# First query–key row by feature chunks, an aligned big buffer and earlier third-slice weights in a graph-attention layer

## The chip, the cores and the metric

One Trainium2 chip; the kernel runs on one core. The metric is the device time of one execution, in microseconds, as the median of the runs. The unchanged kernel took 2683.31 us (three runs, 2682.59 to 2688.69).

## The reference

A pre-norm graph attention layer over 128 graphs of 128 nodes with 768 features, 12 heads of 64:

```
h = relu(layernorm(x))                       # x: [128, 128, 768]
q, k, v = h @ Wq + bq, h @ Wk + bk, h @ Wv + bv
scores = q k^T / sqrt(64) + beta * adj       # per head
scores = where(adj > 0, scores, -9e15)
out = x + softmax(scores) v
```

Everything is float32.

## The kernel before

**Groups and slices.** Four graphs form a group (32 groups). For each group the projections are done in three slices in this order: `qk0` (features 0 to 383 of q and k), `v` (all of v) and `qk1` (features 384 to 767 of q and k). For groups 1 to 31 each slice is done as 15 products of sums of blocks (`product_z`, line 559 holds its matmuls): its weight operands (`T...`) were prepared once, most are kept in DRAM (`kept_...`) and streamed back for each group, eleven stay resident. Group 0 is done plainly (`plain_slice`, matmuls on line 855) from the raw weights, and while it runs VectorE (DVE) and GpSimd (POOL) prepare the operands of the products (`prepare`, lines 283 to 326: `sums` on lines 305 and 307, `rest` on lines 284 to 293, which also stores the operand to DRAM).

**Raw weights.** One big SBUF buffer, `sbig` (line 168), holds the raw q and k weights of the first slice in its first half, the raw v weights in its second half, then the first two graphs of x and a 128x128 identity and averaging matrix. A weight load covers 32 partitions (a quarter, index `a`), so each set of columns takes four DMAs (`load_cols`, line 229). Before the change the first slice is loaded by column block j, 128 columns of all 768 features at a time: per DMA 32 partitions of six 512-byte runs, 96 KB (`raw_qk`, lines 238 to 244, called on lines 344, 345 and 347). The q part of block 0 goes out on the SyncE queue (SP), its k part on the ScalarE queue (ACT), all the rest on SP. The load of graphs 2 and 3 (`load_x(0, 1)`) stands between block 1 and block 2. When the first slice is done, its half of `sbig` is overwritten with the raw weights of the third slice, in eight DMAs (`raw_qk1_piece`, line 246), one each at slots 5 to 12 of the `v` slice (line 1058). A slot is one (row, j, k) step of `plain_slice`; a slice of group 0 has 18.

**The first slice of group 0.** Row r is a pair of graphs (256 columns), j a block of 128 output features of q and of k, k one of three chunks of 256 input features. Each (r, j, k) is four matmuls of q and k, and three k's accumulate in one pair of PSUM banks; there are four such pairs (`take`, `give`). Before the change row 0 goes j by j: j = 0 with all three k's for graph 0, then the same for graph 1, then j = 1 and j = 2 for both graphs. Graphs 0 and 1 are normalized by rows (`rows_1`, `rows_2`: statistics, scaling on DVE, transposes on TensorE line 925, ReLU on ACT line 931). Graphs 2 and 3 are normalized by moments: statistics on DVE (line 364), a first matmul with the averaging matrix (`moments_1`, line 375), a few small DVE operations, a second one (`moments_2`, line 389), a power on POOL (line 396) and the shift (398), then scaling on DVE and ACT (456, 450), and three 32x32 block transposes on DVE (471) that make the operands A10, A11, A12 of row 1. `second` (line 952) turns the biases (three small DMAs on ACT, lines 947 to 949; transpose on TensorE line 957) and is issued in the midst of j = 0.

**Order.** In this first slice the order is the program's with some `issue_after` ties; from the second slice on the order is written out by hand (`manual_schedule`, line 1052) through `then(slot, ...)`. `fill` (line 937) issues matmuls of the identity with itself while TensorE has nothing to do yet: 15 at the start and 1, 1 and 7 after the transposes of graph 0 (`FILL`, line 107).

Of the kernel before, what the change touches and what calls it, by code (L numbers as in the profile page):

```python
# [106 lines left out]
FILL = (1, 1, 7)  # L107
# [21 lines left out]
def direct(ctx, tc, x, adj, wq, bq, wk, bk, wv, bv, beta, out, bad):  # L129
# [36 lines left out]
    RAW = NC * 6 * P  # L166
    sbig = const.tile([P, 2 * RAW + 2 * D + 2 * P], F32, name="sbig")

# [36 lines left out]
    nhalf = const.tile([P, 1], F32, name="nhalf")  # L205
# [3 lines left out]
    tiny = const.tile([P, 1], F32, name="tiny")  # L209
# [3 lines left out]

    NS = 2 * NG + 1
    seen = const.tile([P, NS], F32, name="seen")

# [12 lines left out]
    def load_cols(engine, t, name, at, chunks=slice(0, NC)):  # L229
        for a in range(NB):  # L230
            engine.dma_start(t[a * SQ:(a + 1) * SQ], rows_of[name][a][:, chunks, at:at + t.shape[-1]])

# [5 lines left out]
    def raw_qk(u, t, parts, engines=(nc.sync, nc.sync)):  # L238

        v = t.rearrange("p (c i j n) -> p c i j n", c=NC, i=2, j=3)  # L240
        for lo, hi in parts:
            for i, name in enumerate(("q", "k")):
                load_cols(engines[i], v[:, :, i, lo:hi].rearrange("p c j n -> p c (j n)"), name, (lo + 3 * u) * P)
        name_raw(u, v)
# [8 lines left out]
    def raw_v():  # L253
        t = flat(RAW, RAW + NC * 4 * P).rearrange("p (c n) -> p c n", c=NC)
        own = flat(RAW + NC * 4 * P, 2 * RAW).rearrange("p (c n) -> p c n", c=NC)
        load_cols(nc.sync, t, "v", 0)
        load_cols(nc.sync, own, "v", 4 * P)
        for k in range(3):
            for j in range(3):
                b = t[:, :, j * 2 * P:(j + 1) * 2 * P] if j < 2 else own  # L260
                wt["v", f"B{k}{j}"] = b[:, 2 * k:2 * k + 2].rearrange("p c (i n) -> p c i n", i=2)
# [95 lines left out]
    st, pm, rstd, shift = {}, {}, {}, {}  # L357
# [11 lines left out]
    def moments_1(G, lo, hi):  # L369
# [4 lines left out]
        for q in range(0, P, HD):  # L374
            nc.tensor.matmul(pm[G, lo][q:q + HD, 0], mean8.rearrange("p a i -> p (a i)")[:, q:q + HD],
                             halves(G, lo, hi, 1), start=True, stop=True)
# [8 lines left out]
    def moments_2(G, lo, hi, mean, d):  # L385

        n = hi - lo
        for q in range(0, P, HD):
            nc.tensor.matmul(pm[G, lo][q:q + HD, 1], mean8.rearrange("p a i -> p (a i)")[:, q:q + HD], d,
# [911 lines left out]
```

## Time and profile before

| | |
|---|---|
| median of three runs | 2683.31 us (2682.59 to 2688.69) |
| the profiled execution | 2680.71 us, of which the span from the first to the last instruction is 2678.9 us |
| TensorE busy | 2652.9 us, 99% of the span |
| VectorE, ScalarE, GpSimd busy | 2179.0, 1749.4 and 2072.5 us |
| granted TensorE clock | 0.998 of full speed over the span |
| DMA | 721.71 MB, mean 269 GB/s |

The profile is one execution. In a timeline row stand the start in us, the busy time in us, the engine, the source line, the operation, its output and inputs by name, the form and the count, and in brackets how long the engine sat idle before it and what released it. TensorE's matmuls are PE, its weight loads PEld, the DMA issues of SyncE and ScalarE SPq and ACTq. One float32 matmul shows as two PE rows. A row of a window table has the busy time (and the count) of each engine in one stretch, the granted clock, the mean busy share of the DMA engines, and GB/s.

### The profile page before, as it was taken

To read this page: it belongs to the slowest core of one execution; us is meant where nothing else is said; L and a number is where in the kernel's file an instruction comes from. 1 tells how busy PE (TensorE), PEld (TensorE's weight loads), DVE (VectorE), ACT (ScalarE), POOL (GpSimd) and SP (SyncE) were. 2 spreads that over 40 slices of the span, in tenths; PEclk is the share of its full clock that TensorE was granted. 3 is DMA by queue.
4 is the path that set the end of the run, shared out by engine and by line. 5 is a ranking of instruction groups with operands and counts; after the bars stand their busy time and mean duration, and the time that the engine had idled before them with its cause. 6 is when DMAs were issued, how large, how long until landed. Compare 5 with 4: busy or idle time off the path is not lost.

```text
span 2678.9 us, 121522 instructions
## 1 busy us (share of the span) xinstructions
PE 2652.9 (99%) x52051; PEld 2564.7 (96%) x52051; DVE 2179.0 (81%) x2701; ACT 1749.4 (65%) x4608; POOL 2072.5 (77%) x3043
## 2 busy tenths in 40 slices
PE   9999999999999999999999999999999999999998
PEld 8799999999999999999999999999999999999997
DVE  6877888878888788888788887788887888877885
ACT  2567766676666677666766666776667676667654
POOL 5877778877778777788777787777887777877774
PEclk9999999999999999999999999999999999999999
DMA  9888888989888998889898888988898988888875
GB/s 238 283 261 282 275 270 277 277 265 284 276 271 273 267 279 273 273 277 279 265 281 279 270 272 271 283 274 270 277 277 266 283 277 271 272 274 276 257 240 163
DMA packets 530341, 721.71 MB, mean 269 GB/s; under 512 B 105980, under 2 KB 374024, under 8 KB 529800
## 3 DMA queue, kind: packets, MB, share of 16 engines
q1 hardware_dynamic: 528640, 713.12, 86.7%
q8 instruction: 411, 6.73, 1.0%
q10 hardware_dynamic: 1160, 0.79, 0.2%
q14 instruction: 130, 1.06, 0.1%
HBM read 647.73 MB, written 66.05 MB: 266 GB/s over the span
## 4 chain that ended last, share of the span: by engine, by line
PE 45%; POOL 29%; ACT 13%; issue 5%; DMA 4%; DVE 3%; SPq 0%; POOLq 0%; ACTq 0%; DVEq 0%
PE pair L559 34%; PE pair L695 4%; POOL v L616 4%; PE pair L638 3%; POOL v L615 3%; PE pair L855 3%; POOL A L481 3%; POOL home L614 3%; ACT x L450 3%; ACT e L648 3%; POOL home L601 2%; POOL home L603 2%; ACT home L577 2%; ACT home L579 2%; POOL v L612 2%
## 5 line engine op out<-in xcount | busy, mean ns | idle before, releaser
L583 DVE TENSOR_TENSOR home<-home,pair 128x896 f32<-128x896 f32 x810 | 860.7, 1076 | 273.4 <-PE pair L559 220.7
L559 PE MATMUL pair<-sbig,T_qk 128*64 128x128 f32 x13020 | 833.0, 273 | 1.8 <-DVE sbig L476 0.9
L559 PEld LDWEIGHTS pair<-sbig,T_qk 128*64 128x64 f32 x13020 | 708.2, 137 | 11.6 <-issue 6.4
L559 PE MATMUL pair<-A,T_qk 128*64 128x128 f32 x6944 | 465.6, 273 | 0.4 <-ACT e L707 0.4
L601 POOL TENSOR_TENSOR home<-home 128x256 f32<-128x256 f32 x298 | 246.5, 827 | 268.6 <-DVE home L583 260.1
L678 ACT ACTIVATE e<-e,sm 128x64 f32<-128x64 f32 x1512 | 382.2, 346 | 109.5 <-DVE sm L666 109.5
L559 PE MATMUL pair<-T_v,sbig 128*64 128x128 f32 x6944 | 415.1, 274 | 0.6 <-DMA T_v<-kept_v 0.3
L695 PE MATMUL pair<-v,e 128*64 128x65 f32 x6048 | 401.7, 221 | 6.3 <-DVE e L646 5.9
L577 ACT ACTIVATE home<-pair 128x640 f32<-128x640 f32 x325 | 231.4, 712 | 262.5 <-PE pair L559 201.6
L559 PEld LDWEIGHTS pair<-T_v,sbig 128*64 128x64 f32 x6944 | 380.7, 137 | 12.9 <-issue 10.6
L559 PEld LDWEIGHTS pair<-A,T_qk 128*64 128x64 f32 x6944 | 377.2, 137 | 5.4 <-ACT e L707 4.8
L695 PEld LDWEIGHTS pair<-v,e 128*64 128x64 f32 x6048 | 355.9, 137 | 16.4 <-DVE e L646 12.7
L559 PE MATMUL pair<-sbig,res_qk 128*64 128x128 f32 x4340 | 288.3, 273 | 0.0
L604 POOL TENSOR_TENSOR home<-home 128x256 f32<-128x256 f32 x298 | 238.2, 799 | 23.4
L602 POOL TENSOR_TENSOR home<-home 128x256 f32<-128x256 f32 x298 | 229.8, 771 | 23.4
L559 PEld LDWEIGHTS pair<-sbig,res_qk 128*64 128x64 f32 x4340 | 234.5, 137 | 5.3 <-issue 5.2
L705 ACT ACTIVATE sm<-pair,tiny 128x8 f32<-128x8 f32 x189 | 49.4, 261 | 284.6 <-PE pair L695 284.5
L450 ACT ACTIVATE x<-x,block 128x192 f32<-128x192 f32 x480 | 232.0, 554 | 0.0
L603 POOL TENSOR_TENSOR home<-home 128x128 f32<-128x128 f32 x298 | 213.4, 716 | 23.4
L646 DVE SCALAR_TENSOR_TENSOR e<-pair,biasT 128x1024 f32<-128x1024 f32 x189 | 225.0, 1216 | 2.9 <-PE pair L638 2.8
L648 ACT ACTIVATE e<-e 128x1024 f32<-128x1024 f32 x189 | 193.8, 1066 | 50.2 <-DVE e L646 46.9
L481 POOL TENSOR_TENSOR A<-A 128x256 f32<-128x256 f32 x186 | 168.6, 906 | 56.5 <-DVE A L471 56.5
(201 smaller groups left out, 4598.8 us busy)
## 6 DMA issues: line engine op xcount, KB each, us to landing
T_qk<-kept_qk SPq DMA_DIRECT2D x713, 448.0 KB, 4.8
T_v<-kept_v SPq DMA_DIRECT2D x341, 448.0 KB, 5.6
xo<-in_x_dram SPq DMA_DIRECT2D x189, 256.0 KB, 4.9
out_dram<-xo SPq DMA_DIRECT2D x189, 256.0 KB, 6.0
x<-in_x_dram SPq DMA_DIRECT2D x248, 192.0 KB, 6.2
sbig<-in_x_dram SPq DMA_DIRECT2D x116, 384.0 KB, 3.4
kept_qk<-prep_qk SPq DMA_DIRECT2D x23, 448.0 KB, 3.1
adj<-in_adj_dram SPq DMA_DIRECT2D x128, 64.0 KB, 3.4
```

The costliest lines, as they stand in the source:

```text
L450: nc.scalar.activation(t, t, AF.Relu, bias=shift[G, n], scale=rstd[G, n])
L481: e.tensor_tensor(t[:, 0:2], t[:, 7:8].to_broadcast([P, 2, P]), t[:, 5:7], ALU.subtract)
L559: nc.tensor.matmul(p[q:q + HD, at, :], lhs[:, q:q + HD], rhs, start=(first and at % 4 == 0), stop=True, skip_group_check=True)
L577: nc.scalar.activation(t[:, 0:5], p[:, 0:5], AF.Copy, scale=float(sign))
L583: nc.vector.tensor_tensor(t, t, p[:, 0:7], op)
L601: e.tensor_tensor(t[:, 1:4:2], t[:, 1:4:2], twice(5), ALU.add)
L602: e.tensor_tensor(t[:, 2:5:2], t[:, 2:5:2], twice(1), ALU.add)
L603: e.tensor_tensor(t[:, 4], t[:, 4], t[:, 6], ALU.add)
L604: e.tensor_tensor(t[:, 0:7:6], t[:, 0:7:6], twice(2), ALU.add)
L648: trailing.append(lambda: nc.scalar.activation(e, e, AF.Exp, scale=1.0 / ISCALE))
L678: nc.scalar.activation(o[:, r, b, 0:HD], pa[:, r, b, 0:HD], AF.Copy, scale=t[:, 1, r, b:b + 1])
L695: nc.tensor.matmul(pa[q:q + HD, 2 * g + i, :], k[:, q:q + HD], vt[G, "v", r, h // 4][:, 4 * g + h % 4, :], start=True, stop=True, skip_gro ...
```

## The change

1. `FILL` goes from (1, 1, 7) to (1, 1, 2): five filling matmuls fewer behind the third transposes.
2. The raw weights of the first slice are loaded by chunks k of 256 input features, all 384 columns at once: per DMA 32 partitions of two 1536-byte runs, again 96 KB, again four for q and four for k per chunk. The k part goes out in the order of quarters 2, 3, 0, 1. Queues as before (chunk 0: q on SP, k on ACT; the rest on SP); graphs 2 and 3 of x stand again between the second and the third set.
3. The raw v weights are loaded in four DMAs of 3072-byte runs in place of four of 2048 and four of 1024 bytes.
4. Three small tiles are allocated ahead of `sbig`. Its first byte in a partition was 16,544 (160 over a multiple of 256) and is now 16,896 (a multiple of 512).
5. Row 0 of the first slice is a function of its own, `first_row`. It holds three bank pairs, one for each j, and goes chunk by chunk: k = 0 for graph 0 with the transposes of graph 1 between the j's, k = 0 for graph 1, the biases (`second`), then k = 1 and k = 2 for both graphs. The first moments matmul stands behind (k = 1, j = 1), the second behind (k = 1, j = 2). All transposes of graph 1, the biases and both moments share the one pair that is left.
6. Three of the steps that prepare operands (the sums TX, T9, T12) are put ahead of the statistics of graphs 2 and 3 on DVE.
7. The eight loads of the third slice's raw weights are issued at slots 4, 4, 5, 5, 6, 6, 7, 7 of the `v` slice in place of slots 5 to 12.

Loading graphs 0 and 1 of x by halves on two queues (lines 196 to 200) stands in both kernels.

```
-FILL = (1, 1, 7)
+FILL = (1, 1, 2)
...
+    seen = const.tile([P, NS], F32, name="seen")
+    nhalf = const.tile([P, 1], F32, name="nhalf")
+    tiny = const.tile([P, 1], F32, name="tiny")
     sbig = const.tile([P, 2 * RAW + 2 * D + 2 * P], F32, name="sbig")
...
+    def load_rows(engine, t, name, cols, chunks, order=range(NB)):
+        for a in order:
+            engine.dma_start(t[a * SQ:(a + 1) * SQ], rows_of[name][a][:, chunks, cols])
+
+    def raw_qk0(k, engines=(nc.sync, nc.sync)):
+        c = slice(2 * k, 2 * k + 2)
+        for i, name in enumerate(("q", "k")):
+            load_rows(engines[i], qk0_raw[:, c, i].rearrange("p c j n -> p c (j n)"), name, slice(0, 3 * P), c,
+                      ((0, 1, 2, 3), (2, 3, 0, 1))[i])
...
-    raw_qk(0, flat(0, RAW), ((0, 1),), (nc.sync, nc.scalar))
-    raw_qk(0, flat(0, RAW), ((1, 2),))
+    raw_qk0(0, (nc.sync, nc.scalar))
+    raw_qk0(1)
     load_x(0, 1)
-    raw_qk(0, flat(0, RAW), ((2, 3),))
+    raw_qk0(2)
...
+    def first_row(todo):
+        banks = [take() for _ in range(3)]
+        order = []
+        for j in range(3):
+            order += [("one", 0, 0, j), ("rows", j)]
+        order += [("fold",), ("todo", 0)] + [("one", 0, 1, j) for j in range(3)] + [("second",)]
+        order += [("two", 1, 0), ("two", 1, 1), ("todo", 1, 2, 3), ("two", 1, 2), ("todo", 4), ("two", 2, 0), ("two", 2, 1),
+                  ("todo", 5, 6), ("two", 2, 2), ("todo", 7, 8)]
...
+                elif what == "fold":
+                    folded()
+                    for _ in range(3):
+                        behind_rows(step, 1)
...
+                else:
+                    k, j = args[0], args[-1]
+                    at = slice(args[1] * N, (args[1] + 1) * N) if what == "one" else slice(0, H2)
+                    a, b, p = A[0, f"A0{k}"], wt["qk0", f"B{k}{j}"], banks[j][:, :, 0:H2]
+                    for i in range(2):
+                        for c in range(2):
+                            last = nc.tensor.matmul(p[:, i, at], b[:, c, i], a[:, c, at], start=(k == c == at.start == 0),
+                                                    stop=(c == 1), skip_group_check=True)
...
-    plain_slice(0, "qk0", todo)
+    plain_slice(0, "qk0", todo, (1,), 9, first_row(todo))
...
-        then(5 + n, raw_qk1_piece, n)
+        then(4 + n // 2, raw_qk1_piece, n)
```

On TensorE, in row 0, before the change: the last transposes of graph 1 (line 925), the biases (957), what is left of j = 0 (A00, A01, A02 are chunks k = 0, 1, 2 of the activations; pair1 is j = 0, pair3 is j = 1), and the two moments matmuls (375, 389) side by side behind j = 1.

```order
L925 MATMUL pair0_73<-sbig_77,rows_1_238 128x128 x2
L957 MATMUL pair2_75<-sbig_77,bqk_rows_146 128x12
L855 MATMUL pair1_74<-A02_0_218,sbig_77 128x128 x4
L855 MATMUL pair1_74<-A00_0_200,sbig_77 128x128 x4
L855 MATMUL pair1_74<-A01_0_206,sbig_77 128x128 x4
L855 MATMUL pair1_74<-A02_0_218,sbig_77 128x128 x4
L855 MATMUL pair3_76<-A00_0_200,sbig_77 128x256 x4
L855 MATMUL pair3_76<-A01_0_206,sbig_77 128x256 x4
L855 MATMUL pair3_76<-A02_0_218,sbig_77 128x256 x4
L375 MATMUL pair0_73<-st_0_273,sbig_77 64x16 x2
L389 MATMUL pair0_73<-dev_0_8_300,sbig_77 64x16 x2
```

The same engine and place in the changed kernel (pair1, pair2 and pair3 are j = 0, 1 and 2; line 913 is the transposes, 950 the biases, 373 and 387 the moments).

```order
L913 MATMUL pair0_73<-sbig_80,rows_1_225 128x128 x2
L1065 MATMUL pair3_76<-A00_0_196,sbig_80 128x128 x4
L913 MATMUL pair0_73<-sbig_80,rows_1_225 128x128 x2
L1065 MATMUL pair1_74<-A00_0_196,sbig_80 128x128 x4
L1065 MATMUL pair2_75<-A00_0_196,sbig_80 128x128 x4
L1065 MATMUL pair3_76<-A00_0_196,sbig_80 128x128 x4
L950 MATMUL pair0_73<-sbig_80,bqk_rows_146 128x12
L1065 MATMUL pair1_74<-A01_0_202,sbig_80 128x256 x4
L1065 MATMUL pair2_75<-A01_0_202,sbig_80 128x256 x4
L373 MATMUL pair0_73<-st_0_255,sbig_80 64x16 x2
L1065 MATMUL pair3_76<-A01_0_202,sbig_80 128x256 x4
L387 MATMUL pair0_73<-dev_0_8_299,sbig_80 64x16 x2
```

The biases moved behind all of k = 0, and a block of four matmuls now stands between the two moments matmuls, with all of k = 2 behind the second one.

On DVE, before the change, from the scaling of graph 1 (line 920) to the first moments operations:

```order
L920 TENSOR_SCALAR rows_238<-sbig,mvrow_1_224,rsrow_228 128x256 x3
L966 TENSOR_REDUCE fold<-sbig 128x32
L967 TENSOR_SCALAR sbig<-fold 128x128
L364 BN_STATS st_273<-x_1_129 128x6 x8
L378 TENSOR_REDUCE mean_8_298<-pair_73 128x8
```

and in the changed kernel:

```order
L908 TENSOR_SCALAR rows_225<-sbig,mvrow_1_215,rsrow_219 128x256 x3
L944 TENSOR_REDUCE fold<-sbig 128x32
L945 TENSOR_SCALAR sbig<-fold 128x128
L304 TENSOR_TENSOR prep_qk_4_249<-sbig 128x2x256
L302 SCALAR_TENSOR_TENSOR prep_qk_0_251<-prep_qk_4_249,sbig 128x2x256
L302 SCALAR_TENSOR_TENSOR prep_qk_1_253<-prep_qk_4_249,sbig 128x2x256
L362 BN_STATS st_255<-x_1_129 128x6 x8
L376 TENSOR_REDUCE mean_8_297<-pair_73 128x8
```

Three preparing operations came in ahead of the statistics; they stood behind the transposes of row 1 before.

On the SP queue, before the change, in the `v` slice (line 249 loads the third slice's raw weights, 293 stores prepared operands, 413 loads a row of x):

```order
L249 DMA sbig<-in_L_gnn_Wq_dram 32x6x384
L293 DMA kept_v_655<-prep_v_648 128x896
L293 DMA kept_v_664<-prep_v_657 128x896
L249 DMA sbig<-in_L_gnn_Wq_dram 32x6x384
L249 DMA sbig<-in_L_gnn_Wk_dram 32x6x384
L249 DMA sbig<-in_L_gnn_Wq_dram 32x6x384
L293 DMA kept_v_711<-prep_v_685 128x896
L249 DMA sbig<-in_L_gnn_Wk_dram 32x6x384
```

and in the changed kernel, a little earlier in the same slice:

```order
L249 DMA sbig<-in_L_gnn_Wq_dram 32x6x384
L249 DMA sbig<-in_L_gnn_Wk_dram 32x6x384
L290 DMA kept_v_605<-prep_v_598 128x896
L249 DMA sbig<-in_L_gnn_Wq_dram 32x6x384
L249 DMA sbig<-in_L_gnn_Wk_dram 32x6x384
L290 DMA kept_v_626<-prep_v_619 128x896
L290 DMA kept_v_635<-prep_v_628 128x896
L411 DMA A_1_529<-in_x_dram 128x768
L249 DMA sbig<-in_L_gnn_Wq_dram 32x6x384
L249 DMA sbig<-in_L_gnn_Wk_dram 32x6x384
L290 DMA kept_v_651<-prep_v_644 128x896
```

The last load of the third slice's weights now stands ahead of six of the eleven stores of prepared v operands; before the change it stood ahead of four.

More of the change, by code (lines that the diff above doesn't have):

```diff
@@ L355, in direct @@
     bv_b = const.tile([P, D], F32, name="bv_b")
-    st, pm, rstd, shift = {}, {}, {}, {}
+    st, pm, rstd, shift, first = {}, {}, {}, {}, {}
     def stats(G, g):
@@ L854, in plain_slice @@
                                         behind.enter_context(tc.issue_after(row0.ins))
-                                    last = nc.tensor.matmul(p[q, i, at], lhs[:, q], rhs, start=(k == 0 and c == 0),
+                                    last = nc.tensor.matmul(p[q, i], lhs[:, q], rhs, start=(k == 0 and c == 0),
                                                             stop=(c == 1), skip_group_check=True)
@@ L861, in plain_slice @@
                                              stop=True, skip_group_check=True)
-                    if at is not parts[-1]:
-                        if k == 1:
-                            with tc.issue_after(last.ins):
-                                second()
-                        continue
                     if k == 2:
@@ L911, in rows_1, with rows_2 @@
         return mv, r
[L913 removed]
+    def rows_2(g, mv, r, ks=range(3)):
         v = xg[0, g].rearrange("p b (c j) -> p c b j", c=NC)
[L916 removed]
+        for k in ks:
             if not k:
```

73 lines of the change are left out of this document (37 added, 36 removed).

## The prediction

> **What bounds the kernel now.** I read the busy times first, then the window table, then TensorE's rows in the opening, then what those rows wait for. The page's first part:
>
> ```profile
> span 2678.9 us, 121522 instructions
> PE 2652.9 (99%) x52051; PEld 2564.7 (96%) x52051; DVE 2179.0 (81%) x2701; ACT 1749.4 (65%) x4608; POOL 2072.5 (77%) x3043
> ```
>
> Two stretches of the window table, whose columns are the stretch, its length, the busy time and count of PE, PEld, DVE, ACT and POOL, the granted clock, the DMA engines' share and GB/s:
>
> ```profile
> 31.00:46.00 15.00, 15.00 (x70) 13.22 (x71) 14.96 (x39) 2.34 (x6) 9.55 (x11) 1.00 1.02 233
> 46.00:82.00 36.00, 36.00 (x164) 28.51 (x162) 33.54 (x81) 12.23 (x28) 30.98 (x48) 1.00 0.93 304
> ```
>
> TensorE is the bound: 26 us of the span are not covered by it. From 31 to 82 us it has no idle time at all. So the change can earn only what it takes out of the first 31 us, plus small waits later, and what it takes out there reaches the end if nothing later becomes late. TensorE's rows of the opening, from the timeline:
>
> ```profile
> 1.50 6.52 PE L939 MATMUL pair<-sbig 128*128 128x128 f32 x30 [1.50 <-POOL sbig masks.py:199]
> ...
> 8.96 1.73 PE L939 MATMUL pair<-sbig 128*128 128x128 f32 x14
> 10.52 1.95 PE L855 MATMUL pair<-A,sbig 128*128 128x128 f32 x16
> 12.31 0.82 PE L925 MATMUL pair<-sbig,rows 128*128 128x128 f32 x6
> 14.76 0.20 PE L957 MATMUL pair<-sbig,bqk_rows 12*128 12x12 f32 x1 [1.64 <-DMA bqk_rows<-in_L_gnn_bk_dram]
> 14.89 9.02 PE L855 MATMUL pair<-A,sbig 128*128 128x128 f32 x56
> 23.84 0.29 PE L375 MATMUL pair<-st,sbig 128*64 128x16 f32 x4
> 25.11 0.29 PE L389 MATMUL pair<-dev,sbig 128*64 128x16 f32 x4 [0.97 <-DVE dev L382]
> 25.33 21.33 PE L855 MATMUL pair<-A,sbig 128*128 128x256 f32 x96
> ...
> 30.85 3.32 PEld L855 LDWEIGHTS pair<-A,sbig 128*128 128x128 f32 x16 [0.47 <-DVE A L471]
> ```
>
> Row 0 starts at 10.52, waits 1.64 for the biases and 0.97 between the two moments matmuls, and row 1 starts at 30.86, when DVE delivers its first transposed operand. What leads to that operand:
>
> ```profile
> 18.51 2.18 DVE L364 BATCH_NORM_STATS2 st<-x 128x6 f32<-128x192 f32 x8 [7.17 <-DMA x<-in_x_dram]
> 25.91 1.68 POOL L396 TENSOR_TENSOR rstd<-ve,nhalf 128x8 f32<-128x8 f32 x1 [10.46 <-DVE ve L394]
> 27.91 1.40 DVE L456 TENSOR_SCALAR x<-x,rstd,shift 128x192 f32<-128x192 f32 x4 [2.08 <-POOL shift L398]
> 30.09 1.90 DVE L471 STREAM_TRANSPOSE A<-x 128x512 f32<-128x512 f32 x3
> ```
>
> The statistics were over at 20.7; the moments waited 3.1 us for their turn on TensorE. From the second moments matmul (25.11) to row 1 (30.86) it takes 5.75 us.
>
> **The change part by part.** *Fewer fills.* 14 PE rows from 8.96 to 10.52 are 0.111 us each; five fills are ten of them, 1.1 us. TensorE could begin row 0 at 9.4.
>
> *Weights.* Does the first set land by then? The chain of waits, which gives start and duration of each link:
>
> ```profile
> 1.35 5.13 DMA sbig<-in_x_dram
> ...
> 6.50 4.11 DMA sbig<-in_L_gnn_Wk_dram
> ```
>
> The two graphs of x are in at 6.48 and the first set of weights, eight DMAs of 96 KB, at 10.6: 768 KB at 190 GB/s. Their rows among the DMA issues, then windows:
>
> ```profile
> sbig<-in_L_gnn_Wq_dram SPq DMA_DIRECT2D x12, 96.0 KB, 4.4
> sbig<-in_L_gnn_Wq_dram SPq DMA_DIRECT2D x4, 288.0 KB, 5.9
> ```
>
> ```profile
> 3.00:4.00 1.00, 1.00 (x6) 1.00 (x6) 0.00 (x0) 0.00 (x0) 0.00 (x0) 1.00 1.11 298
> 9.00:10.00 1.00, 1.00 (x12) 1.00 (x11) 0.32 (x2) 0.49 (x2) 0.56 (x1) 1.00 1.23 175
> 15.00:16.00 1.00, 1.00 (x10) 1.00 (x11) 0.00 (x0) 0.16 (x1) 0.20 (x1) 1.00 1.17 233
> 44.00:48.00 4.00, 4.00 (x20) 3.52 (x19) 3.01 (x9) 0.84 (x2) 3.68 (x8) 1.00 1.01 408
> ```
>
> 298 is x by partition halves on two queues, 175 the weights in 512-byte runs with q and k on the same quarter of the partitions, 233 graphs 2 and 3 in 768-byte runs, 408 transfers over all partitions. The new loads have longer runs, an aligned buffer and, in the first set, q and k on opposite halves. No row shows just that, so it is bounded by 190 (nothing gained: weights at 10.6, row 0 at 10.2 since its k part is needed only 0.45 later) and 298 (768 KB in 2.6 us, weights at 9.1, so the fills bind). I take 235, nearest to the 233 of 15 to 16 us: the set takes 3.3 us and lands at 9.8; its k part is needed at 9.4 + 0.45, so row 0 starts at 9.4.
>
> Here the Trainium skill speaks against the change: "SBUF — State Buffer", section "Can I just issue two DMAs to hit both halves?", says two such transfers serialize and measured only 6% over one. By 6% alone the set would land at 10.4 and row 0 begin at 9.95. The rows 298 against 175 here lean the other way, though their run lengths differ too. In favour, "DMA: Bandwidth & Descriptors", section "How a descriptor splits into AXI transactions", has a run that starts off a 256-byte boundary cost extra beats: by its count a 512-byte run 160 bytes off costs 21 beats for 16, which would be an estimated 24% off the weights' 4.1 us, landing at 9.6. No run here separates alignment.
>
> *Row 0's work* is the same in both kernels: 48 PE rows of 128 columns at 0.111 and 48 of 256 columns at 0.222 (21.33 over 96), 16.0 us; transposes 0.7, biases 0.1, two moments at 0.24: 17.3. In the new order nothing of it should wait. The biases' turn comes behind k = 0, at 9.4 + 5.3 + 0.7 = 15.4, and they were in at 14.76. Between the two moments matmuls DVE needs at most 25.11 less 23.84, 1.3 us, and four matmuls of 256 columns, 1.8 us, now lie there. So 1.64 and 0.97 go, and TensorE is done with row 0 at 26.7. The one shared pair of banks makes each transpose of graph 1 wait for the ReLU of the one before; 0.9 us of matmuls lie between, and a ReLU takes 0.32 (0.94 for three):
>
> ```profile
> 11.69 0.28 ACTq L949 DMA_DIRECT2D bqk_rows<-in_L_gnn_bk_dram  x1
> 12.73 0.94 ACT L931 ACTIVATE A<-pair 128x256 f32<-128x256 f32 x3 [3.18 <-PE pair L925]
> ```
>
> The bias DMAs stand ahead of these ReLUs on ACT, and their issue ended at 11.97. If it ends no sooner, the second transpose comes at about 12.4 where its turn is at 11.5: 0 to 0.9 us lost. I take 0.1, since each of these issues follows a landing of weights, and those come sooner.
>
> *The moments.* The first comes behind k = 0 and two blocks of k = 1, at 9.4 + 6.1 + 3.6 = 19.1, the second 2.0 later, at 21.1, and 5.75 after that row 1 can start: 26.9, just behind TensorE's own 26.7. That needs the statistics over by 19.1, so x in by 16.9 in place of 18.4. From 6.48 to 18.4 three sets of 768 KB were loaded, 198 GB/s; at 235 they take 10.0 and x is in at 16.5. The second set is then in at 13.2, and the three preparing operations that now stand ahead of the statistics need it:
>
> ```profile
> 31.91 0.65 DVE L307 TENSOR_TENSOR prep_qk<-sbig 128x512 f32<-128x512 f32 x1
> 33.08 1.28 DVE L305 SCALAR_TENSOR_TENSOR prep_qk<-prep_qk,sbig 128x512 f32<-128x512 f32 x2
> ```
>
> They end at 15.1, in time. With the 0.1 from above and 0.3 for signals between engines I put **row 1 at 27.3, 3.55 us sooner**.
>
> *Later.* DVE and POOL start their preparation with TensorE's row 1, so as much sooner, and DVE another 1.9 us lighter. The third slice's weights:
>
> ```profile
> 85.67 3.67 PE L855 MATMUL pair<-A,sbig 128*64 128x256 f32 x32
> ...
> 86.20 0.69 DVE L307 TENSOR_TENSOR prep_qk<-sbig 128x512 f32<-128x512 f32 x1 [4.32 <-DMA sbig<-in_L_gnn_Wk_dram]
> ...
> 118.27 1.60 DVE L476 TENSOR_TENSOR sbig<-A,A 128x896 f32<-128x896 f32 x1 [2.10 <-POOL A L483]
> ...
> 133.08 1.75 PE L559 MATMUL pair<-sbig,T_qk 128*64 128x128 f32 x28 [0.92 <-DVE sbig L476]
> ```
>
> The last of them came at 86.2, half a microsecond behind TensorE's first product of that slice, so a lead of 3.55 would have met them. Sent one to five slots sooner (a slot is 2.2 us: 85.67 less 46.66, over 18) the last should be in some 10 us ahead, and DVE need not idle 4.32. The 2.10 of DVE behind POOL at 118 and TensorE's 0.92 at 133 come from the same backlog; between 0 and 0.92 of that goes, and I take 0.4, since a mask (L646) that follows TensorE stands ahead of the last sums. After that the order is unchanged. The v weights in four longer loads cost nothing: TensorE enters that slice at 46.66, inside the stretch from 46 without idle time, and row 1's 16 us stand ahead of it; without that cover their lateness would be a wait there.  The buffer's new address could touch all products, but a matmul takes 273 ns with its weights from `A` (a multiple of 256) and from `sbig` (not), so I take nothing; a difference under the rows' last digit, 1 ns in 273 on the 0.83 ms of line 559's first row, would be 3 us either way:
>
> ```profile
> L559 PE MATMUL pair<-sbig,T_qk 128*64 128x128 f32 x13020 | 833.0, 273 | 1.8 <-DVE sbig L476 0.9
> L559 PE MATMUL pair<-A,T_qk 128*64 128x128 f32 x6944 | 465.6, 273 | 0.4 <-ACT e L707 0.4
> ```
>
> **Sum:** 3.55 + 0.4, about 4.0 us. The profiled execution took 2680.71, 1.8 more than its span, so it would take 2676.7. It lay 2.6 below the median of the runs, 2683.31, from which I predict **2679.3**.
>
> **The rivals.**
> *Weights land no sooner.* For it: runs of 512 and of 768 bytes differ by 175 to 233 alone, and both are far from 408. Row 0 starts at 10.2; x in at 18.4, statistics over at 20.7, first moments there, four matmuls, the second at 22.75, row 1 at 28.5: 2.35 + 0.4 gained, 2680.6. (The Trainium skill's sentence on two halves, above, leads about here.)
> *The lead is given back by 133 us.* Eight loads of 288 KB at some 200 GB/s are 11.8 us, now crowded among the stores of prepared v operands; DVE's buffers come free later and TensorE waits for the sums. Against it: DVE has 4.32 + 2.10 + 1.9 us in hand. Gain 0 to 1: 2682.8.
> *Slower: the clock falls.* With five fills gone TensorE stands idle from 9.4 until the weights land. The first 30 fills took 0.217 us a row, later ones 0.111, so it starts at half rate; if the gap throws it back for as long as at the start (6.5 us), 3.25 us are lost, on top of the first rival's late weights: 2683.9. It decides only where the gap is longer than the 1.64 before the biases, behind which the rows still took 0.112; the weights would have to land past 11.0.
> *More than forecast.* Later waits shrink too:
>
> ```profile
> 1000.00:2000.00 1000.00, 996.59 (x20130) 973.30 (x20128) 822.88 (x968) 676.02 (x1785) 793.76 (x1155) 1.00 0.89 274
> ```
>
> 3.4 us in 1000 leaves room for 5 to 8 gained in all, 2677.
>
> **How the numbers follow.** Forecast 0.58, weights no sooner 0.20, given back 0.12, clock 0.03, more 0.07. The forecast's own range is 2678 to 2680.5; the runs before spread from 2682.6 to 2688.7 round a median that lay 2.6 above the profiled execution. The range 2675.5 to 2683.5 takes in all but the clock and a very large gain. A difference of 0.3%, 8 us, is about what a measurement of this kernel can tell from no change; more than the opening holds would be needed: faster 0.06, same 0.90, slower 0.04.
>
> **What would show it.** Right: the first matmul of row 0 near 9.5, no wait at the biases, the second moments matmul near 21.4 without a wait, row 1 near 27.3, products of group 1 some 4 us sooner, DVE's 4.32 wait gone. Wrong: statistics starting at 18 or later; a ReLU late behind the bias DMAs; a new wait of TensorE between 43 and 135 us; rows of row 0 at 0.2 us.

## The result and the profile after

The changed kernel took 2680.31 us (median of 22 runs, 2676.51 to 2686.40), the kernel before 2684.80 us (22 runs on the same chips): a ratio of 0.9985, 95% interval 0.9979 to 0.9991. The forecast was 2679.3. So it is 0.15% faster: the interval excludes a ratio of 1, but the difference is smaller than the spread of single runs of one kernel, 8.5 and 9.9 us. The profiled execution took 2679.08 us in place of 2680.71, with spans of 2677.2 and 2678.9: 1.6 and 1.7 us apart, where the medians stand 4.5 apart. Both numbers matter below.

TensorE's rows of the changed kernel, from the timeline:

```profile
9.05 1.06 PE L1065 MATMUL pair<-A,sbig 128*128 128x128 f32 x8
...
15.36 0.23 PE L950 MATMUL pair<-sbig,bqk_rows 12*128 12x12 f32 x1
15.51 3.72 PE L1065 MATMUL pair<-A,sbig 128*128 128x256 f32 x16
20.54 0.29 PE L373 MATMUL pair<-st,sbig 128*64 128x16 f32 x4 [1.30 <-DVE st L362]
20.76 1.99 PE L1065 MATMUL pair<-A,sbig 128*128 128x256 f32 x8
22.68 0.29 PE L387 MATMUL pair<-dev,sbig 128*64 128x16 f32 x4
...
28.43 15.81 PE L849 MATMUL pair<-A,sbig 128*128 128x256 f32 x72
...
102.95 4.11 PE L849 MATMUL pair<-A,sbig 128*64 128x256 f32 x36 [0.39 <-ACT home L866]
...
121.34 6.28 PE L557 MATMUL pair<-sbig,T_qk 128*64 128x128 f32 x112
...
131.13 1.75 PE L557 MATMUL pair<-sbig,T_qk 128*64 128x128 f32 x28 [0.79 <-DVE sbig L474]
```

Row 0 starts 1.47 us sooner (9.05 for 10.52), and the waits for the biases (1.64) and between the two moments matmuls (0.97) are gone. A new one, 1.30, stands before the first moments matmul: the statistics are late. Row 1 starts at 28.43, 2.43 us ahead of before. At the products of group 1 the lead is 1.82 (121.34 for 123.16), at the sum that VectorE delivers late in both kernels 1.95 (131.13 for 133.08).

VectorE in the same kernel: the statistics, row 1's transposes, the waits for the third slice's weights and for stores of prepared operands, and the transposes of group 1's bias, on which much hangs below:

```profile
18.21 2.18 DVE L362 BATCH_NORM_STATS2 st<-x 128x6 f32<-128x192 f32 x8 [2.66 <-DMA x<-in_x_dram]
...
27.67 1.90 DVE L469 STREAM_TRANSPOSE A<-x 128x512 f32<-128x512 f32 x3
...
80.21 0.69 DVE L304 TENSOR_TENSOR prep_qk<-sbig 128x512 f32<-128x512 f32 x1 [2.25 <-DMA sbig<-in_L_gnn_Wk_dram]
82.66 0.91 DVE L302 SCALAR_TENSOR_TENSOR prep_qk<-prep_qk,sbig 128x512 f32<-128x512 f32 x1 [0.90 <-DMA kept_v<-prep_v]
84.84 0.69 DVE L304 TENSOR_TENSOR prep_qk<-sbig,prep_qk 128x512 f32<-128x512 f32 x1 [1.26 <-DMA kept_v<-prep_v]
...
100.62 0.70 DVE L497 STREAM_TRANSPOSE biasT<-adj 128x512 f32<-128x512 f32 x1
```

The statistics show x in at 18.21, 0.3 us sooner than before (18.51), where 16.5 was forecast. The weights of the first set did come sooner: the first bias load, issued on ScalarE when their last part lands, went out at 8.96 in place of 10.64. What follows them hardly did. SyncE's issues in the changed kernel, then the end of its chain of waits up to x (start and duration; a DMA's duration runs to its landing), then windows of the opening in the kernel before and in the changed one (the last two columns are the DMA engines' share and GB/s):

```profile
7.15 1.72 SPq L237 DMA_DIRECT2D sbig<-in_L_gnn_Wq_dram  x4
8.92 1.97 SPq L237 DMA_DIRECT2D sbig<-in_L_gnn_Wk_dram  x4
10.94 2.48 SPq L196 DMA_DIRECT2D x<-in_x_dram  x4
```

```profile
9.39 3.14 DMA sbig<-in_L_gnn_Wk_dram
12.53 0.02 issue
12.55 0.37 SPq L196
12.92 0.04 issue
12.96 5.06 DMA x<-in_x_dram
```

```profile
9.00:13.00 4.00, 4.00 (x38) 3.89 (x36) 1.63 (x6) 0.76 (x3) 0.56 (x1) 1.00 1.14 186
```

```profile
9.00:13.00 4.00, 4.00 (x36) 3.83 (x36) 1.58 (x5) 1.18 (x4) 1.00 (x3) 1.00 0.69 186
13.00:18.00 5.00, 5.00 (x35) 4.57 (x34) 1.98 (x3) 0.34 (x2) 0.20 (x1) 1.00 0.91 232
```

Both kernels move 186 GB/s from 9 to 13 us. Before, the DMA engines were full (1.14); now they are a third idle (0.69): the same bytes cost them less, but no more bytes went through. SyncE sends the four loads of 96 KB from 8.92 on 0.49 us apart (four in 1.97), which is 200 GB/s. Among the four of x it pauses: the issue at 12.55 waits for a load of the second set, sent at 9.39, to land. The last load of x, sent at 12.96, then takes 5.06 to land, while the DMA engines are 0.91 busy. Other runs speak against the issue as what holds x: in the kernel before with only the buffer moved, the issues of x start 1.4 us sooner (11.16 for 12.57) and x is in at the same 18.51. What did hold it, no run shows by itself.

The trace's DMA packets show where the time went. Those of x are the only ones of 768 bytes in this stretch. 96% of them were through at 16.04 (17.03 before), but the last one only at 17.20 (17.66 before), and 0.33 MB of other loads (0.16 MB before) had moved between the first and the last. So x's bulk came 1.0 us sooner, its last pieces 0.5, in company with the third set of weights, which was issued behind it.

Where the lead stops counting shows in the chain of waits from 28 to 135 us, by line: first the kernel before, then the changed one.

```profile
by line: PE pair L855 74.6%; PE pair L559 5.9%; PE pair L860 5.9%; PE pair L638 3.1%; PE pair L695 2.6%; DVE xo L723 1.4%; issue 1.3%; DVE x L456 1.3%; DVE e L646 1.1%; DVE sbig L476 0.9%; DVE A L471 0.7%; DVE x L458 0.6%; PE pair L375 0.2%
```

```profile
by line: issue 9.7%; POOL prep_v L286 6.2%; DMA kept_qk<-prep_qk 6.1%; POOL prep_v L287 5.6%; DVE prep_qk L304 5.5%; POOL prep_qk L286 5.0%; DVE sbig L474 4.5%; POOL prep_qk L287 4.4%; POOL A L479 4.3%; DMA x<-in_x_dram 4.0%; DVE st L362 4.
```

Before, nine tenths of that chain is TensorE. In the changed kernel it runs through GpSimd's and VectorE's preparation of operands and the stores behind it, and TensorE hardly appears (some 4%). Two variants below lie between: with only the buffer moved in the kernel before it is still TensorE (91%), with the quarters straight TensorE has 42%.

### The profile page after: what moved, and what is told of

Same layout as the page of the kernel before. It is cut to its first block, busy times and chain, and to the rows that moved or that the text cites. A ratio compares the mean times of both kernels' runs of the same rounds, so it can differ in the third digit from the quotient of the medians.

```text
span 2677.2 us, 121501 instructions
## 1 busy us (share of the span) xinstructions
PE 2652.1 (99%) x52041; PEld 2563.4 (96%) x52041; DVE 2179.3 (81%) x2701; ACT 1747.9 (65%) x4608; POOL 2070.9 (77%) x3043
## 4 chain that ended last, share of the span: by engine, by line
PE 39%; POOL 33%; ACT 13%; issue 6%; DMA 4%; DVE 4%; SPq 0%; POOLq 0%; ACTq 0%; DVEq 0%
PE pair L557 33%; POOL v L614 4%; PE pair L693 4%; POOL A L479 3%; POOL v L613 3%; POOL home L612 3%; PE pair L636 3%; ACT x L448 3%; ACT e L646 3%; POOL home L599 2%; POOL home L601 2%; ACT home L575 2%; ACT home L577 2%; POOL v L610 2%; POOL home L611 2%
## 5 line engine op out<-in xcount | busy, mean ns | idle before, releaser
L557 PEld LDWEIGHTS pair<-sbig,T_qk 128*64 128x64 f32 x13020 | 708.4, 137 | 11.4 <-issue 6.6
L557 PEld LDWEIGHTS pair<-T_v,sbig 128*64 128x64 f32 x6944 | 380.9, 137 | 12.3 <-issue 10.5
```

The costliest lines, as they stand in the source:

```text
L557: nc.tensor.matmul(p[q:q + HD, at, :], lhs[:, q:q + HD], rhs, start=(first and at % 4 == 0), stop=True, skip_group_check=True)
```

## The experiments

"Row 1" is the start of its transposes on VectorE, "sum" the start of the matmuls that wait for VectorE's sum near 131 us; both from the one profiled execution. Ratios are to the kernel before, run on the same chip. Two profiled executions are no typical ones: that of "before, third sooner" took 2692.0, the longest of its eleven, and that of "buffer back" 2683.19, 1.4 over its median.

| kernel | median us (runs) | ratio, 95% interval | row 1 | sum |
|---|---|---|---|---|
| before | 2684.80 (22) | | 30.09 | 133.08 |
| before, again | 2685.22 (1) | | 30.24 | 133.24 |
| changed | 2680.31 (22) | 0.9985 (0.9979 to 0.9991) | 27.67 | 131.13 |
| changed, again | 2680.47 (11) | 0.9987 (0.9978 to 0.9996) | 27.70 | 131.65 |
| quarters straight | 2678.90 (11) | 0.9986 (0.9977 to 0.9995) | 28.24 | 131.50 |
| seven fills | 2680.54 (11) | 0.9989 (0.9980 to 0.9998) | 28.15 | 131.35 |
| buffer back | 2681.77 (11) | 0.9991 (0.9981 to 1.0001) | 27.73 | 137.68 |
| third slice late | 2684.89 (11) | 1.0001 (0.9992 to 1.0010) | 27.42 | 134.68 |
| bias sooner | 2682.07 (11) | 0.9992 (0.9983 to 1.0001) | 27.23 | 131.66 |
| before, buffer moved | 2682.26 (11) | 0.9992 (0.9983 to 1.0001) | 28.92 | 131.66 |
| before, third sooner | 2685.09 (11) | 1.0006 (0.9997 to 1.0015) | 29.79 | 137.06 |

**The changed kernel again, and the kernel before again.** No edit.

> The changed kernel as it is, once more, to see which of its times repeat. Theory A (the gain is what the opening and the first 135 us show): row 0 starts at 9.05 us again, row 1 at 28.4, the products of group 1 at 121.3, each within 0.2, and the time stands 2 to 2.5 us under the kernel before (ratio near 0.9992). Theory B (the whole run gains, for instance by the buffer's address, since the medians of 22 runs each stand 4.5 us apart where the two profiles show only 1.7 to 2.4): ratio near 0.9984, and idle time of TensorE between 135 and 2600 us clearly under the 8.9 us before.

> The kernel before as it is, once more, for its profile. Theory A (its executions differ by what TensorE loses between 95 and 135 us, and the profile shown was a good one): a wait of TensorE for line 877 near 105 us of 1 to 4 us, products of group 1 at 124 to 127 in place of 123.16, and a span of 2680 to 2683. Theory B (they differ elsewhere): no such wait, products at 123.2 within 0.3, and what the span adds lies between 135 and 2600 us.

The changed kernel's ratio, 0.9987, lies between those of the two theories. The opening and the first 135 us repeat, roughly as theory A had them: row 1 within 0.03 and 0.15 us, the sum within 0.5 and 0.2, with no wait of TensorE for line 877 in the kernel before. Within 0.2 it was not throughout: row 0 of the changed kernel started at 9.39 for 9.05, its products at 121.69 for 121.34. From the sum to the end of the span the two executions of the kernel before took 2545.8 and 2550.2 us, those of the changed one 2546.1 and 2548.6. So single executions scatter by 2 to 4 us behind the sum, in a stretch that both kernels run in the same order. Theory B of the first run wanted TensorE's idle time from 135 to 2600 us clearly under the 8.9 of before. It was 8.8 and 10.5 in the changed kernel, 8.9 and 11.0 in the kernel before, so the profiles show no gain there. Theory B of the second run held for the products and the missing wait; of the 4.5 us that its span adds, 2.1 are idle time of TensorE from 135 to 2600.

**The k part in the order of quarters 0, 1, 2, 3.**

```
-                      ((0, 1, 2, 3), (2, 3, 0, 1))[i])
+                      ((0, 1, 2, 3), (0, 1, 2, 3))[i])
```

> The changed kernel, but the k part of the raw weights goes out in the order of quarters 0, 1, 2, 3, as the q part does. The first set landed by 9 us in the changed kernel, 10.6 before. Theory A (opposite halves at the same time make the set fast): the set lands near 10.5 and row 0 starts at 10.0 to 10.2 in place of 9.05; the first moments matmul still stands at 20.5, since its statistics wait for x, which is no later, so row 1 stays at 28.4 and the time does not move. Theory B (the longer runs or the aligned buffer make it fast): row 0 starts at 9.05 as before, nothing changes. Time 2680 by both, within 1.

The first bias load, issued when the set has landed, and TensorE's rows:

```profile
9.83 0.40 ACTq L935 DMA_DIRECT2D beta_c<-in_L_gnn_beta_dram  x1
```

```profile
9.64 1.13 PE L1065 MATMUL pair<-A,sbig 128*128 128x128 f32 x8 [0.29 <-ACT A L919]
```

The set lands at 9.83 in place of 8.96 (8.78 to 9.15 in five executions with the new order): opposite quarters at the same time are worth some 0.9 us of 3.3 behind x, a quarter, by one execution of the old order. The Trainium skill, "SBUF — State Buffer", section "Can I just issue two DMAs to hit both halves?", has 6%; here the measurement decides, and the order was worth more. Theory A was right about row 0 in the main (9.64, 0.6 later; it said 10.0 to 10.2) and about the time, which did not move; row 1 moved 0.6 and not 0, since x came 0.6 later too.

**The small tiles behind the big buffer again, and ahead of it in the kernel before.** Two kernels, one for each direction:

```
-    seen = const.tile([P, NS], F32, name="seen")
...
     sbig = const.tile([P, 2 * RAW + 2 * D + 2 * P], F32, name="sbig")
+    seen = const.tile([P, NS], F32, name="seen")
```

> The changed kernel with the three small tiles behind the big buffer again, so that it starts 160 bytes over a multiple of 256. Theory A (the address matters to DMAs alone): the first set lands up to 0.6 us later, row 0 starts by 9.05 to 9.6, row 1 at 28.4 to 28.6, time within 0.5 of the changed kernel. Theory B (the address matters to TensorE's reads and so to the whole run): a matmul on line 557 with its weights from the buffer takes visibly over 273 ns or TensorE's idle time grows, and the time is 2 us or more over the changed kernel. Theory C: nothing moves at all.

> The kernel before with the three small tiles ahead of the big buffer and nothing else changed, so that the buffer starts at a multiple of 512 bytes. Still open is why the runs of the changed kernel lie 4 us under those of the kernel before while the profiles show 1.4 to 2 us at the sum near 131 us, after which both do the same. Theory A (the address helps the loads and stores of the whole run): the first set lands at 10.0 or sooner in place of 10.6, the time from the sum near 133 us to the end is 2547 us or less in place of 2546 to 2550, and the median is 2 us under the kernel before. Theory B (the address changes nothing): the first set lands at 10.4 to 10.8, row 1 starts at 30.4 to 30.9, the sum comes at 133, the time within 1 us of the kernel before, and the 2 us stay open or are the scatter of single executions.

The kernel before with the buffer moved: the first bias load, TensorE at the biases, row 1's transposes, the late sum.

```profile
9.72 0.38 ACTq L947 DMA_DIRECT2D beta_c<-in_L_gnn_beta_dram  x1
```

```profile
13.60 0.20 PE L957 MATMUL pair<-sbig,bqk_rows 12*128 12x12 f32 x1 [0.64 <-ACT A L931]
```

```profile
28.92 1.90 DVE L471 STREAM_TRANSPOSE A<-x 128x512 f32<-128x512 f32 x3
```

```profile
131.66 1.75 PE L559 MATMUL pair<-sbig,T_qk 128*64 128x128 f32 x28 [0.67 <-DVE sbig L476]
```

The address alone brings the set in 0.9 us sooner (9.72 for 10.64), takes 1.0 off the wait for the biases, and puts row 1 1.17 and the sum 1.42 ahead. Its runs lie 1.5 us under those of the kernel before (2683.73, 15 runs beside it), but the interval of the ratio includes 1. Theory A was right about the set and near about the time, but not about the way: from the sum to the end it took 2550 us, no less than before. What the profile shows of the address lies in the opening. The Trainium skill's count of beats ("DMA: Bandwidth & Descriptors", section "How a descriptor splits into AXI transactions"), from which the prediction worked out an estimate of 9.6, fits the 9.72 measured here.

In the other direction, with the longer runs, the set lands 0.5 us later (9.44) and row 1 stays (28.50 on TensorE), as theory A said. A matmul of line 557 with its weights from the buffer takes 273 ns in both, so theory B finds nothing in TensorE's reads. But this execution lost 6.5 us by the sum. VectorE, then TensorE, then windows with the granted clock in the third column from the end:

```profile
100.81 1.92 DVE L304 TENSOR_TENSOR prep_qk<-prep_qk,sbig 128x512 f32<-128x512 f32 x2 [2.26 <-DMA kept_qk<-prep_qk]
102.66 0.94 DVE L304 TENSOR_TENSOR res_qk<-prep_qk,sbig 128x512 f32<-128x512 f32 x1
103.63 0.82 DVE L304 TENSOR_TENSOR res_qk<-res_qk,sbig 128x512 f32<-128x512 f32 x1
104.38 0.70 DVE L497 STREAM_TRANSPOSE biasT<-adj 128x512 f32<-128x512 f32 x1
```

```profile
106.70 7.03 PE L849 MATMUL pair<-A,sbig 128*64 128x256 f32 x36 [4.07 <-ACT home L866]
```

```profile
104.00:105.00 1.00, 0.00 (x0) 0.00 (x0) 1.00 (x2) 0.00 (x0) 0.00 (x0) 1.00 0.87 341
107.00:112.00 5.00, 5.00 (x26) 2.68 (x24) 5.00 (x10) 1.32 (x3) 4.61 (x8) 0.50 0.01 4
113.00:115.00 2.00, 2.00 (x34) 1.47 (x32) 2.00 (x3) 0.30 (x1) 1.84 (x4) 1.00 0.63 258
```

VectorE waits 2.26 for a store, does group 1's bias transposes 3.8 us later (104.38 for 100.62), ScalarE's squares wait for those with the emptying of a bank queued behind them, and TensorE waits 4.07 for the bank. Then its clock falls to half, and 36 rows take 7.03 in place of 4.11. The median, 2681.77, 1.3 us over the changed kernel's, leaves room for this in some executions only. That the address caused it is not shown.

**The third slice's weights at slots 5 to 12 again, and sooner in the kernel before.**

```
-        then(4 + n // 2, raw_qk1_piece, n)
+        then(5 + n, raw_qk1_piece, n)
```

> The changed kernel with the eight loads of the third slice's raw weights at slots 5 to 12 again. Theory A (as predicted, the later loads would meet the lead): TensorE enters the third slice at 83.25 and waits there for weights that land near 84 to 85.5, 0.5 to 2 us, so the products of group 1 start at 122 to 123 and the time is 0.5 to 2 us over the changed kernel. Theory B (TensorE never needed them that soon, only DVE did): no wait of TensorE between 80 and 90 us, products at 121.3 to 121.8, time the same, and DVE's wait for Wk is 4 us or more where the changed kernel had 2.2.

> The kernel before with the eight loads of the third slice's raw weights at slots 4, 4, 5, 5, 6, 6, 7, 7 and nothing else changed. The other seven edits without this one gave 2684.9, no gain over the kernel before. Theory A (this edit only keeps a lead that the opening earns): row 1 at 30.86, VectorE's wait for Wk goes down from 4.3 by about 2, products of group 1 at 122.8 to 123.2, time within 1 us of the kernel before. Theory B (this edit is the gain by itself): the time is 3 us or more under the kernel before, products at 119 to 120.

Without this edit all the others are worth nothing: 2684.89. VectorE, then TensorE, then a window with the granted clock, of the changed kernel with late loads:

```profile
84.28 0.69 DVE L304 TENSOR_TENSOR prep_qk<-sbig 128x512 f32<-128x512 f32 x1 [6.55 <-DMA sbig<-in_L_gnn_Wk_dram]
```

```profile
104.94 5.79 PE L849 MATMUL pair<-A,sbig 128*64 128x256 f32 x36 [2.39 <-ACT home L866]
```

```profile
107.00:109.00 2.00, 2.00 (x14) 1.06 (x12) 2.00 (x4) 0.00 (x0) 1.84 (x4) 0.50 0.39 152
```

Theory B was right that VectorE waits for the weights (6.55) and TensorE does not. Neither had what follows from it: VectorE's bias transposes come 2 us later (102.61), so TensorE waits 2.39 us for the bank, 20 us behind the slice's start, and pays 1.7 more in clock. The sum comes at 134.68. And alone, in the kernel before, the edit earns nothing either (2685.09). In its profiled execution VectorE waits twice for stores of prepared v operands, among which the loads now stand, and the bank comes 1.41 late:

```profile
82.64 0.69 DVE L307 TENSOR_TENSOR prep_v<-sbig,prep_v 128x512 f32<-128x512 f32 x1 [3.97 <-DMA kept_v<-prep_v]
92.26 0.69 DVE L307 TENSOR_TENSOR prep_qk<-sbig,prep_qk 128x512 f32<-128x512 f32 x1 [4.31 <-DMA kept_v<-prep_v]
```

```profile
106.10 4.11 PE L855 MATMUL pair<-A,sbig 128*64 128x256 f32 x36 [1.41 <-ACT home L877]
```

Theory A held there for the time; its 122.8 to 123.2 for the products did not (124.49). The gap of 1.41 left the 36 rows at 4.11, the one of 2.39 above did not.

**Seven fills again.**

```
-FILL = (1, 1, 2)
+FILL = (1, 1, 7)
```

> The changed kernel with seven filling matmuls behind the third transposes again in place of two, so that row 0 starts 1.1 us later. Theory A (x and its statistics bound row 1; TensorE waited 1.2 to 1.3 us for them at the first moments matmul): row 0 at 10.2 to 10.5, the wait before the moments shrinks to 0 to 0.3, row 1 at 28.4 to 28.6, and the time does not move: the five fills taken away earn nothing. Theory B (TensorE's own start bounds row 1, as the prediction had it): row 1 at 29.4 to 29.6 and the time 1 us over the changed kernel.

Row 0 started at 10.23, the wait before the moments shrank only to 0.80 since x came 0.5 later in this execution, row 1 came at 28.92 on TensorE, 0.5 later like x, and the time is that of the changed kernel (2680.54). Theory A held in the main: the five fills taken away earn nothing.

**Group 1's bias sooner.**

```
-    bias(1, 4, 6, 8)
+    bias(1, 2, 6, 8)
```

> The changed kernel with one number changed: the first step of group 1's bias (the transposes on line 497 of VectorE and, behind them, the squares on line 498 of ScalarE) at slot 2 of the third slice in place of slot 4. In the changed kernel VectorE does those transposes at 100.6 us, behind sums that wait for stores of prepared operands; ScalarE's squares wait for them 6.6 us with the emptying of a bank (line 866) queued behind, and TensorE waits 0.39 for that bank, 0.70 in the same kernel run again, 4.07 with the buffer at its old address. Theory A (this chain is where the opening's lead is lost, by an amount that differs from execution to execution): no wait of TensorE for line 866 near 103 us, products of group 1 at 120.9 to 121.3, the time 0.5 to 1.5 us under the changed kernel. Theory B (VectorE's backlog as a whole sets it): the wait moves to the next thing VectorE owes, at 110 to 133 us, and products and time stay.

TensorE:

```profile
120.30 3.23 PE L557 MATMUL pair<-sbig,T_qk 128*64 128x128 f32 x56
...
124.55 3.28 PE L557 MATMUL pair<-sbig,T_qk 128*64 128x128 f32 x56 [1.02 <-DMA T_qk<-kept_qk]
...
131.66 1.75 PE L557 MATMUL pair<-sbig,T_qk 128*64 128x128 f32 x28 [1.11 <-DVE sbig L474]
```

Theory A was right about the wait for the bank, which is gone, and the products start 1.0 us sooner. Theory B was right about the rest: TensorE waits the difference back, on a streamed operand and on the same sum at 131.66, and the time is not under the changed kernel's.

**Loads over all partitions.** Three kernels; the first for the opening, the second for the third slice, the third for both with the bias sooner.

```
+        all_of[name] = w.rearrange("(a c j) n -> c a j n", a=NB, j=SQ)
...
-            load_rows(engines[i], qk0_raw[:, c, i].rearrange("p c j n -> p c (j n)"), name, slice(0, 3 * P), c,
-                      ((0, 1, 2, 3), (2, 3, 0, 1))[i])
+            for c in (2 * k, 2 * k + 1):
+                engines[i].dma_start(qk0_raw[:, c, i].rearrange("p j n -> p (j n)"), all_of[name][c][:, :, 0:3 * P])
```

> The changed kernel, with the raw weights of the first slice and graphs 2 and 3 of x loaded in transfers over all 128 partitions: per set of weights four DMAs of 192 KB (128 runs of 1536 bytes) in place of eight of 96 KB over 32 partitions, and x in eight of 96 KB (128 runs of 768 bytes) in place of four of 192 KB. The same bytes. Theory A (transfers over a quarter of the partitions hold x up at some 205 GB/s, and x holds up row 1): x is in by 14 to 15 us in place of 18.2, the wait of 1.2 to 1.3 before the first moments matmul goes, row 1 starts at 27.0 to 27.3. Theory B (the queue or the run length holds x up): x is in at 17.5 to 18.5 and row 1 stays at 28.4. For the time: what is lost between 95 and 131 us does not hang on the opening (row 1 at 28.0, 28.4, 28.9 and 29.0 gave the sum that ends near 131 within 0.5 us), so the time stays at 2680 to 2681 even if row 1 is sooner; if the opening does carry through, 2679.

> The changed kernel, with the raw weights of the third slice loaded in twelve DMAs of 192 KB over all 128 partitions, three each at slots 4 to 7, in place of eight of 288 KB over 32 partitions. The same bytes. Theory A (the transfers from 60 to 85 us keep the DMA engines full, and those over a quarter of the partitions waste their time): VectorE's waits for Wk (2.2 to 3.5 us) and for stores of prepared v operands (1.6 to 2.2) shrink by half or more, its transposes on line 497 come at 97 to 99 in place of 100.6, TensorE's wait for line 866 goes, and the wait for line 474 near 131 begins 0.4 to 1 us sooner; time 0.5 to 1 us under the changed kernel. Theory B (VectorE's and GpSimd's own work sets the pace): these waits of VectorE shrink, but the products near 131 us do not move.

> Both kinds of wide loads, and the bias of group 1 at slot 2 of the third slice. The version that the runs so far point to. Theory A (the opening, the loads and the bias are what stands between TensorE and the products): row 1 at 27.0 to 27.3, no wait for line 866, products of group 1 at 119 to 119.8, the sum near 131 delivered by 130, time 1.5 to 2 us under the changed kernel. Theory B (VectorE's backlog, or the streamed operands that group 1 loads from 115 us on, set the pace): the products start sooner and wait the difference back before 135 us, time 2680 to 2682.

All three were slower: 2705.22 (5 runs; ratio 1.0078, 1.0064 to 1.0092), 2698.76 (5 runs; 1.0051, 1.0037 to 1.0065) and 2718.64 (4 runs; 1.0136, 1.0120 to 1.0153). Windows of the first:

```profile
8.00:12.00 4.00, 1.64 (x13) 1.29 (x11) 2.40 (x9) 1.04 (x3) 0.56 (x1) 1.00 0.27 100
12.00:16.00 4.00, 1.17 (x6) 0.98 (x7) 0.00 (x0) 0.00 (x0) 0.00 (x0) 0.84 0.27 100
16.00:20.00 4.00, 2.47 (x12) 2.17 (x11) 0.00 (x0) 0.00 (x0) 0.00 (x0) 0.50 0.27 100
```

A share of 0.27 is about that of four of sixteen DMA engines (0.25). The source of these loads is four blocks of 32 rows. The Trainium skill, "DMA: Bandwidth & Descriptors", section "Why a DMA increments its semaphore by 16 and not by 1", says that the slowest dimension of the two patterns picks how many engines take part, and four blocks would give four; the trace agrees. So these runs do not test what they were made for, whether a quarter of the partitions or the queue held x up; that stays open, but for what the moved buffer says of the queue's issues (above). What they show is the other direction: weights and x that are late hold up all of row 0, and in the second kernel, where the same 0.27 and 100 GB/s stand from 72 to 76 us, TensorE waits 4.29 us for the third slice's weights and 6.88 for a bank.

No version of these beats the changed kernel by more than the runs scatter.

## Why the prediction was right, and where it was not

*Right: what bounds the kernel before, and the size.* TensorE was the bound up to 131 us in the kernel before, and what the change took out of the first 31 us did move the rest, in part. The forecast gain was 4.0 us; the medians moved by 4.5 (3.5 in the second set of runs, 2680.47 for 2683.93).

*Weights and row 0.* Forecast: set in at 9.8, row 0 at 9.4, bounds of 190 and 298 GB/s. Measured: 8.96 and 9.05; the set was faster than the upper bound. The order of quarters gave 0.9 where it was tried apart, the buffer's address 0.9 in the kernel before and 0.5 in the changed one; what the longer runs gave was not tried apart. The waits at the biases and between the moments went, as said, and from the second moments matmul to row 1 it took the 5.75 us of the sum (22.68 to 28.43).

*The step that failed* is the one on x: "at 235 they take 10.0 and x is in at 16.5". The rate of the first set was carried over to all three sets, though only the first goes out on two queues: from 9 to 13 us it was 186. x came at 18.21, and the new wait of 1.30 before the first moments matmul made row 1 28.43 in place of 27.3: 2.43 us sooner, not 3.55. The runs bear this out: in eight executions with the changed kernel's row 0, x came anywhere from 17.38 to 18.79, and the transposes of row 1 followed it by 9.45 or 9.46 us each time, whether the fills were two or seven and the first set landed at 8.78 or at 9.83. In the kernel before they followed x by 11.4 to 11.6. So x, not TensorE's own work, bounded row 1 in the changed kernel. Why x was late is shown in part only: its last pieces came 1.2 us behind its bulk; the run with the buffer moved speaks against SyncE's pace as the cause, and the company of the third set was not tried apart. What the prediction listed as a sign of being wrong, statistics at 18 or later, is what came.

*Later.* The 0.4 of the wait at 133 us was not earned: 0.79 to 0.98 remain, 1.11 with the bias sooner. Of the lead of 2.43 some 0.5 to 1 was given back by the sum. The rival "given back by 133 us" named stores crowded by the sooner loads as the cause; that is what one profile of the loads alone, in the kernel before, looks like. In the changed kernel they are needed: "DVE need not idle 4.32" became 2.25 to 3.50 for the weights and 1.6 to 2.2 for stores, and without the edit it is 6.55. The prediction's reason, that the loads would meet TensorE's first product of that slice, was wrong in its place: the price falls due at 103 us, through VectorE's bias transposes and a bank. (The v slice is entered at 46.50, not 46.66; the slot stays 2.2 us.)

*Why the size came out all the same.* It did not come out of the forecast's terms, so it is luck as far as the traces go. From before to changed, the sum gains 1.4 to 2.1 us in the profiles. Of the seven executions in the table with row 1 (on VectorE) between 27.23 and 28.24, five have the sum at 131.1 to 131.7, as has the kernel before with only the buffer moved; the other two lost more, by 2.39 and 4.07 us of waiting for a bank and the clock behind it. Once TensorE is some 1.4 us ahead, the chain of waits changes to the preparation by VectorE and GpSimd, which would explain why more lead earns nothing; no run made that preparation shorter. That accounts for some 2 of the 3.5 to 4.5 us between the medians. The rest stays open: behind the sum, four profiles of the kernel before and its variants took 2545.8 to 2553.1 us and seven of the changed kernel and its variants 2543.7 to 2549.1, and these overlap.

*The clock.* The rival did not come true in the changed kernel, whose set came in time and whose longest gap between two matmuls up to 135 us is 1.30. Its mechanism, a gap in TensorE longer than the 1.64 before the biases, showed in two of the variants, at 103 us in place of the start, and at the start only where the wide loads came late (0.50 from 16 to 20 us).

## What to carry to other kernels

When one engine is 99% busy, time taken out of its opening counts only until the next engine's backlog becomes the limit; here that was after a lead of about 1.4 us, where the chain of waits changed from TensorE to GpSimd and VectorE. A cheaper first transfer does not make the ones behind it come sooner by as much: look at when the last piece of each lands, and at the DMA engines' share beside the GB/s. And an edit that earns nothing alone (the sooner loads) can be what keeps the gain of the others, so undo edits one at a time from the changed side too.

## What the runs showed of the hardware

- A gap in TensorE of 1.41 us cost itself alone; gaps of 2.39 and 4.07 us also came with a granted clock of 0.50 for some 3 and 7 us, and the 36 rows took 1.7 and 2.9 us more. The Trainium skill, "TensorE: Matmul & The Clock Gate", section "Why this matters for your kernels", warns of gaps above about 3 us; here 2.39 was enough.
- A load of 128 partitions from four blocks of rows moved 100 GB/s with 0.27 of the DMA engines; with the loads of 32 partitions that they replaced, the stretch from 9 to 18 us moved 186 to 232 with 0.69 to 0.91.
- Moving the buffer from 160 bytes over a multiple of 256 to a multiple of 512 shortened the load of 768 KB behind x by 0.9 us of 4.1 with runs of 512 bytes (10.64 to 9.72), and by 0.5 us with runs of 1536 bytes (9.44 to 8.96).
